# TensorE's unrolled program against a loop of 31 turns, in a gather-and-add kernel

## The chip, the cores and the metric

The kernel runs on one core of one Trainium2 chip. A core has TensorE (matrix products), VectorE (DVE in the profile), ScalarE (Activation, ACT), GpSimd (POOL) and SyncE (SP), each with its own instruction stream; semaphores order them. Sixteen DMA engines move data between the chip's memory (HBM) and the core's SBUF. The metric is the device time of one execution in microseconds, the median of several runs.

## The reference

```
x: (128, 128, 1024) f32     itok: (128,) int32, 0 to 7     weights: (8, 128, 128) f32
w = weights[itok]                                 # one matrix per batch
return x + einsum('bct,bcd->bdt', x, w)
```

For each of the 128 batches, a 128 x 128 matrix is chosen by the batch's subject, its transpose multiplies the batch's 128 x 1024 block, and the block is added. 67.1 MB are read and 67.1 MB written; the weights are 0.5 MB.

## The kernel before

A *slot* holds 4 batches (H * G, with H = 2 halves of G = 2 batches), 128 partitions by 4096 floats, 2 MB. There are SLOTS = 12 of them in SBUF, `xs[0]` to `xs[11]`, and NT = 32 fillings; filling i uses slot k = i % 12. All loops in the Python text are unrolled, so each engine's stream is a straight list.

The loads are issued from the ScalarE queue (`load`, through `transfer`, L59), one per batch, with 16 KB packets. From filling 12 on, ScalarE first waits until the slot's former content has been stored. The stores are issued from the SyncE queue (`store`), one per slot, but one per half in the first and last filling. The very last batch is stored by a transfer of its own, `last`, after the main block.

The work between is in halves, j = 0 to 63. For each half:

- GpSimd reads the subjects into registers (every 16 batches), waits until VectorE has added half j - 2 and, except in the first two halves, until the half's load has landed, and copies each batch's matrix from `w_all` into one of four small tiles `ws` (L202). For this it works out an address in a register, which the trace calls FUSED_REGOPS.
- TensorE waits until the semaphore `s_copied` has reached j + 1 and runs four matrix products of 128 x 512 outputs (L212), two per batch, into one of two PSUM tiles `ps`. The chip runs each f32 product as two pairs of weight load and matmul.
- VectorE waits for `s_product`, adds the half in PSUM to the half in the slot, in place (L223), and raises `s_added`.
- SyncE waits for `s_added` and issues the store.

In the first two halves TensorE also waits for the load itself. Before all this it runs three products on a tile of zeros (L152). The end (L235) waits on the ScalarE queue for the stores of the last 12 fillings.

A slot's place in the address of a matmul is a constant of the unrolled program. With 64 halves of four products, two pairs each, TensorE's stream has 512 weight loads and 512 matmuls of this kind, and each waits for `s_copied` at a constant that grows with j.

Of the kernel before, what the change touches and what calls it, by code (L numbers as in the profile page):

```python
# [30 lines left out]
G = 2  # L31
H = 2

N = 512

SLOTS = 12

W_SLOTS = 4
P_SLOTS = 2
# [12 lines left out]
def transfer(nc, engine, out, in_):  # L52

    later, nc._always_lower_symbolic_ap = nc._always_lower_symbolic_ap, False
    ins, outs = engine.lower_ap_dma(in_), engine.lower_ap_dma(out)
    nc._always_lower_symbolic_ap = later
    return engine.add_instruction(  # L59
        mybir.InstDMACopy(  # L60
            name=nc.get_next_instruction_name(),
            engine=engine.engine,
            ins=ins,
            outs=outs,
            mode="Copy",
            cce_op=ALU.bypass,
            queue=QUEUES[engine.engine],
        )
    )


@with_exitstack
def kernel(
    ctx: ExitStack,
    tc: tile.TileContext,
    x: bass.AP,
    subjects: bass.AP,
    weights: bass.AP,
    out: bass.AP,
):  # L80
    nc = tc.nc
    B, C, T = x.shape
    S, _, D = weights.shape
    NT = B // (G * H)

    def sbuf(name, *shape, dtype=F32):
        return ctx.enter_context(nc.sbuf_tensor(name, list(shape), dtype)).ap()


    room = -(nc.sbuf_base + -nc.sbuf_base % 32) % ALIGN  # L90
    if room:
        sbuf("room", C, room // 4)
    xs = [sbuf(f"x{i}", C, H * G, T) for i in range(SLOTS)]
    given, near, wrap, index = (
        sbuf(name, 1, B, dtype=I32) for name in ("given", "near", "wrap", "index")
    )
    w_all = sbuf("w_all", C, S, D)
    ws = [sbuf(f"w{i}", C, 1, D) for i in range(W_SLOTS)]
    zeros = sbuf("zeros", C, N)
    ps = [  # L100
        ctx.enter_context(nc.psum_tensor(f"ps{i}", [D, G, T], F32)).ap() for i in range(P_SLOTS)
    ]

    s_given = tc.alloc_semaphore("s_given")
    s_wall = tc.alloc_semaphore("s_wall")
    s_index = tc.alloc_semaphore("s_index")
    s_zeros = tc.alloc_semaphore("s_zeros")
    s_copied = tc.alloc_semaphore("s_copied")
    s_product = tc.alloc_semaphore("s_product")
    s_added = tc.alloc_semaphore("s_added")  # L110

    s_pair = [[tc.alloc_semaphore(f"s_pair{i}_{h}") for h in range(H)] for i in range(SLOTS)]


    s_first = tc.alloc_semaphore("s_first")

    def emptied(i, h):

        turns = i // SLOTS
        return (DMA * G + (DMA if h == H - 1 else 0)) * turns  # L120

    def loaded(i, q):

        h = q // G
        return s_pair[i % SLOTS][h], emptied(i, h) + DMA * G

    def load(engine, i, q):
        k, h = i % SLOTS, q // G
        transfer(
            nc,  # L130
            engine,
            xs[k][:, q, :],
            x[i * H * G + q].rearrange("(a r) t -> a (r t)", r=ROWS),
        ).then_inc(s_pair[k][h], DMA)

    def store(i, q0, q1):
        k, b = i % SLOTS, i * H * G
        transfer(
            nc,
            nc.sync,  # L140
            out[b + q0 : b + q1].rearrange("g d t -> d g t"),
            xs[k][:, q0:q1, :].rearrange("d (o g) t -> d o (g t)", g=min(G, q1 - q0)),
        ).then_inc(s_first if i == 0 and q1 == G else s_pair[k][(q1 - 1) // G], DMA)

    with tc.tile_critical():  # L145

        nc.sync.dma_start(given, subjects.rearrange("(o b) -> o b", o=1)).then_inc(s_given, DMA)

        nc.vector.memset(zeros, 0.0).then_inc(s_zeros, 1)  # L149
        nc.tensor.wait_ge(s_zeros, 1)  # L150
        for _ in range(IDLE):
            nc.tensor.matmul(  # L152
                ps[P_SLOTS - 1][:, G - 1, :N], zeros[:, :D], zeros, start=True, stop=True
            )

        nc.vector.wait_ge(s_given, DMA)
        nc.vector.tensor_scalar(near, given, -S, S - 1, ALU.max, ALU.min).then_inc(s_index, 1)  # L159
        nc.vector.wait_ge(s_index, 1)  # L160
        nc.vector.tensor_scalar(wrap, near, 0, S, ALU.is_lt, ALU.mult).then_inc(s_index, 1)  # L161
        nc.vector.wait_ge(s_index, 2)
        nc.vector.tensor_tensor(index, near, wrap, ALU.add).then_inc(s_index, 1)  # L163
        nc.gpsimd.wait_ge(s_index, 3)


        nc.scalar.dma_start(w_all, weights.rearrange("s c d -> c s d")).then_inc(s_wall, DMA)  # L167
        for i in range(NT):
            k = i % SLOTS
            if i == SLOTS:  # L170
                nc.scalar.wait_ge(s_first, DMA)
            if i >= SLOTS:
                nc.scalar.wait_ge(s_pair[k][H - 1], emptied(i, H - 1))
            for q in range(H * G):
                load(nc.scalar, i, q)


        for j in range(NT * H):
            i, q0, q1 = j // H, j % H * G, (j % H + 1) * G
            k = i % SLOTS  # L180
            p = ps[j % P_SLOTS]

            ahead = j < P_SLOTS
            if ahead:
                nc.tensor.wait_ge(*loaded(i, q0))
            for q in range(q0, q1):
                b = i * H * G + q
                if b % R == 0:  # L190
                    _, subject = nc.values_load_multi_w_load_instructions(
                        index[0:1, b : b + R],
                        engines=[mybir.EngineType.Pool],
                        min_val=0,
                        max_val=S - 1,
                        skip_runtime_bounds_check_because="the index is clamped on the chip above",
                    )
                if b == 0:
                    nc.gpsimd.wait_ge(s_wall, DMA)
                if not ahead and q == q0:  # L200
                    nc.gpsimd.wait_ge(s_added, j - P_SLOTS + 1)
                copy = nc.gpsimd.tensor_copy(  # L202
                    ws[b % W_SLOTS], w_all[:, bass.ds(subject[b % R], 1), :]
                )
                if not ahead and q == q0:
                    copy.wait_op(*loaded(i, q0), "sem-ge")
            copy.then_inc(s_copied, 1)

            nc.tensor.wait_ge(s_copied, j + 1)
            for q in range(q0, q1):  # L210
                for t in range(0, T, N):
                    mm = nc.tensor.matmul(  # L212
                        p[:, q % G, t : t + N],
                        ws[(i * H * G + q) % W_SLOTS][:, 0, :],
                        xs[k][:, q, t : t + N],
                        start=True,
                        stop=True,
                    )
            mm.then_inc(s_product, 1)

            mine = xs[k][:, q0:q1, :]
            nc.vector.wait_ge(s_product, j + 1)
            nc.vector.tensor_tensor(  # L223
                mine, p, mine, ALU.add
            ).then_inc(s_added, 1)

            if i == 0 or q1 == H * G or i == NT - 1:
                nc.sync.wait_ge(s_added, j + 1)
                store(i, q0 if i in (0, NT - 1) else 0, q1 - (b == B - 1))

    with tc.tile_critical() as waits:
        for i in range(NT - SLOTS, NT):
            nc.scalar.wait_ge(s_pair[i % SLOTS][H - 1], emptied(i + SLOTS, H - 1))  # L235
        nc.scalar.wait_ge(s_pair[(NT - 1) % SLOTS][0], emptied(NT - 1 + SLOTS, 0) + DMA)
    last = nc.sync.dma_start(out[B - 1], xs[(NT - 1) % SLOTS][:, H * G - 1, :])

    tc.add_manual_dep(
        last.ins,  # L240
        waits.name,
        mybir.DependencyInfo(mybir.DependencyClass.NoSync, mybir.DependencyReason.SCHED_ONLY),
        reason="the end of the program waits for it",
    )
# [27 lines left out]
```

## Time and profile before

| | us |
|---|---|
| median of 3 runs | 325.33 (325.26 to 325.57) |
| the profiled execution, its own time | 325.08 |
| its span, first to last instruction | 323.3 |
| TensorE matmul busy | 239.6 (74%), 518 instructions |
| VectorE busy | 147.9 (46%) |
| GpSimd busy | 34.0 (11%) |

| DMA queue | packets in the span | MB |
|---|---|---|
| q10, loads (ScalarE queue) | 7184 | 67.64 |
| q1, stores (SyncE queue) | 8882 | 67.11 |
| q8, instructions | 4 | 0.07 |
| q14, instructions | 4 | 0.03 |

The profile is of one execution. Its time is 1.8 us more than its span, which counts from the program's first instruction to its last. Matmuls are pipelined, so a busy TensorE is not TensorE at its peak. The page cuts the span into 40 slices of 8.1 us and gives the busy share of each in tenths. "DMA" is the mean over the 16 DMA engines. [...] The trace also holds each DMA packet with its queue, size, start and duration, but not the number of its engine.

### The profile page before, as it was taken

How to read it: one execution, taken by the hardware profiler on the slowest of the kernel's cores; microseconds unless marked ns; L12 is line 12 of the kernel's file. 1: busy time of each engine (PE TensorE's matmuls, PEld its weight loads, DVE VectorE, ACT ScalarE, POOL GpSimd, SP SyncE). 2: the span in 40 equal slices, each digit the busy share in tenths (PEclk: the TensorE clock that was granted, in tenths of full speed). 3: DMA queues.
4: the chain of work that ended last, by engine and by line, in shares of the span. 5: the costliest groups of instructions: out<-in, count | busy, mean ns of one | idle time of the engine just before them, and what ended most of it. 6: DMA issues, size and time to landing. Idle time of an engine off the chain costs nothing.

```text
span 323.3 us, 1608 instructions
## 1 busy us (share of the span) xinstructions
PE 239.6 (74%) x518; PEld 94.5 (29%) x518; DVE 147.9 (46%) x68; POOL 34.0 (11%) x132
## 2 busy tenths in 40 slices
PE   6999988998888888888889988888888587000000
PEld 2444433333333333333333333333333232000000
DVE  1375655555555555555555555555555355000000
POOL 1011111111111111111111011111111010000000
PEclk9999999999999999999999999999999999555555
DMA  7999999999999999999999999999999999999996
GB/s 270 430 381 423 436 419 423 426 428 428 431 423 425 434 415 427 428 429 420 432 430 418 428 425 428 423 430 429 419 435 416 424 427 427 427 424 429 429 423 276
DMA packets 16074, 134.85 MB, mean 417 GB/s; under 512 B 2625, under 2 KB 3650, under 8 KB 3906
## 3 DMA queue, kind: packets, MB, share of 16 engines
q10 hardware_dynamic: 7184, 67.64, 49.9%
q1 hardware_dynamic: 8882, 67.11, 49.3%
q8 instruction: 4, 0.07, 0.1%
q14 instruction: 4, 0.03, 0.0%
HBM read 67.63 MB, written 67.11 MB: 417 GB/s over the span
## 4 chain that ended last, share of the span: by engine, by line
PE 41%; DVE 20%; issue 17%; POOL 4%; DMA 2%; POOLq 1%; ACTq 0%; SPq 0%
PE ps L212 41%; DVE x L223 20%; POOL w L202 4%; DMA x<-in_x_dram 2%; POOLq L202 1%; ACTq L59 0%; ACTq L167 0%; ACTq L268 0%; SPq L145 0%
## 5 line engine op out<-in xcount | busy, mean ns | idle before, releaser
L212 PE MATMUL ps<-x,w 128*128 128x512 f32 x512 | 234.7, 604 | 31.6 <-POOL w L202 30.0
L223 DVE TENSOR_TENSOR x<-ps,x 128x2048 f32<-128x2048 f32 x64 | 146.7, 2292 | 125.4 <-PE ps L212 125.4
L212 PEld LDWEIGHTS ps<-x,w 128*128 128x128 f32 x512 | 92.6, 189 | 173.8 <-issue 92.3
L202 POOL COPY w<-w_all 128x128 f32 x128 | 33.8, 294 | 234.8 <-DMA x<-in_x_dram 204.5
L152 PE MATMUL ps<-zeros 128*128 128x512 f32 x6 | 4.9, 978 | 1.7 <-DVE zeros L149 1.7
L152 PEld LDWEIGHTS ps<-zeros 128*128 128x128 f32 x6 | 1.8, 326 | 3.8 <-issue 2.1
L149 DVE MEMSET zeros<- 128x512 f32 x1 | 0.5, 485 | 1.1 <-SPq L145 1.1
L159 DVE TENSOR_SCALAR near<-given 1x128 int32<-1x128 int32 x1 | 0.2, 216 | 0.6 <-DMA given<-in_itok_B_dram 0.6
L163 DVE CUSTOM_DVE_ANT_0 index<-near,wrap 1x256 uint16<-1x256 uint16 x1 | 0.3, 278 | 0.0
L161 DVE TENSOR_SCALAR wrap<-near 1x128 int32<-1x128 int32 x1 | 0.2, 215 | 0.0
L259 POOL MEMSET const-float32-0.0<- 128x1 f32 x1 | 0.1, 99 | 0.2 <-issue 0.2
L259 POOL MEMSET const-bfloat16-1.0<- 128x1 bf16 x1 | 0.1, 102 | 0.0
L259 POOL MEMSET const-uint8-127<- 128x1 uint8 x1 | 0.1, 102 | 0.0
L259 POOL MEMSET const-float32-1.0<- 128x1 f32 x1 | 0.1, 99 | 0.0
## 6 DMA issues: line engine op xcount, KB each, us to landing
x<-in_x_dram ACTq DMA_DIRECT2D x128, 512.0 KB, 32.0
out_dram<-x SPq DMA_DIRECT2D x30, 2048.0 KB, 47.2
out_dram<-x SPq DMA_DIRECT2D x3, 1024.0 KB, 14.0
out_dram<-x SPq DMA_DIRECT2D x2, 512.0 KB, 21.2
w_all<-in_L_cond_weights_dram ACTq DMA_DIRECT2D x1, 512.0 KB, 4.2
given<-in_itok_B_dram SPq DMA_DIRECT2D x1, 0.5 KB
```

The costliest lines, as they stand in the source:

```text
L149: nc.vector.memset(zeros, 0.0).then_inc(s_zeros, 1)
L152: nc.tensor.matmul(ps[P_SLOTS - 1][:, G - 1, :N], zeros[:, :D], zeros, start=True, stop=True)
L159: nc.vector.tensor_scalar(near, given, -S, S - 1, ALU.max, ALU.min).then_inc(s_index, 1)
L161: nc.vector.tensor_scalar(wrap, near, 0, S, ALU.is_lt, ALU.mult).then_inc(s_index, 1)
L163: nc.vector.tensor_tensor(index, near, wrap, ALU.add).then_inc(s_index, 1)
L202: copy = nc.gpsimd.tensor_copy(ws[b % W_SLOTS], w_all[:, bass.ds(subject[b % R], 1), :])
L212: mm = nc.tensor.matmul(p[:, q % G, t : t + N], ws[(i * H * G + q) % W_SLOTS][:, 0, :], xs[k][:, q, t : t + N], start=True, stop=True,)
L223: nc.vector.tensor_tensor(mine, p, mine, ALU.add).then_inc(s_added, 1)
L259: nc = _bacc.Bacc("TRN2", target_bir_lowering=False, num_devices=1)
```

## The change

The slots become one tile `x_all` of 12 slots, and `xs[i]` are views of it, so that a slot's place can be an offset. The matmuls of a half move into a function `multiply(slot, q0, q1)`. It is called with a constant slot for the first filling, where the two waits for a load stand ahead of it, and in a loop on TensorE, `Fori(1, NT)`, for the 31 others, with the slot `turn % SLOTS` in a register. A turn is one filling: two halves, eight matrix products. Because a wait in a loop cannot grow with j, TensorE now waits until `s_copied` is at least 1 and takes one off it.

The loop stands after the unrolled text of the other engines, whose streams keep their order; each engine's stream gets one more branch at the seam. In TensorE's stream the built program shows, per turn: one register move, two separate semaphore instructions, eight fused register operations (one ahead of each product), the eight products, one addition and one compare-and-branch.

```diff
-    xs = [sbuf(f"x{i}", C, H * G, T) for i in range(SLOTS)]
+    x_all = sbuf("x_all", C, SLOTS * H * G * T)
+    xs = [
+        x_all[:, i * H * G * T : (i + 1) * H * G * T].rearrange("c (q t) -> c q t", t=T)
+        for i in range(SLOTS)
+    ]
...
+    def multiply(slot, q0, q1):
+        p = ps[q0 // G % P_SLOTS]
+
+        nc.tensor.wait_ge(s_copied, 1).then_inc(s_copied, -1)
+        for q in range(q0, q1):
+            for t in range(0, T, N):
+                at = slot * (H * G * T) + (q * T + t)
+                mm = nc.tensor.matmul(
+                    p[:, q % G, t : t + N],
+                    ws[q % W_SLOTS][:, 0, :],
+                    x_all[:, bass.ds(at, N)],
+                    start=True,
+                    stop=True,
+                )
+        mm.then_inc(s_product, 1)
...
-            nc.tensor.wait_ge(s_copied, j + 1)
-            for q in range(q0, q1):
-                for t in range(0, T, N):
-                    mm = nc.tensor.matmul(
-                        p[:, q % G, t : t + N],
-                        ws[(i * H * G + q) % W_SLOTS][:, 0, :],
-                        xs[k][:, q, t : t + N],
-                        start=True,
-                        stop=True,
-                    )
-            mm.then_inc(s_product, 1)
+            if i == 0:
+                multiply(0, q0, q1)
...
+        with nc.tensor.Fori(1, NT) as turn:
+            for h in range(H):
+                multiply(turn % SLOTS, h * G, (h + 1) * G)
```

## The prediction

> **What bounds the kernel now.** I read the page's slices first, to see which resource is full and until when.
>
> ```profile
> PE   6999988998888888888889988888888587000000
> DMA  7999999999999999999999999999999999999996
> GB/s 270 430 381 423 436 419 423 426 428 428 431 423 425 434 415 427 428 429 420 432 430 418 428 425 428 423 430 429 419 435 416 424 427 427 427 424 429 429 423 276
> q8 instruction: 4, 0.07, 0.1%
> q14 instruction: 4, 0.03, 0.0%
> ```
>
> The 16 DMA engines are full from the second slice to the last but one, at about 427 GB/s, while TensorE stops six slices (48 us) before the end. What follows TensorE's stop is a backlog of stores. So the bytes over the rate set the time, and TensorE matters only if it lets the queues run dry. Next the waits, for what TensorE itself waits on.
>
> ```profile
> POOL w L202 <- DMA x<-in_x_dram: 204.5, 55, 6.8
> DVE x L223 <- PE ps L212: 125.4, 64, 8.8
> PE ps L212 <- POOL w L202: 30.0, 55, 3.7
> ```
>
> GpSimd, which copies the weight matrices for TensorE, waits for loads 55 times, 204.5 us in all; TensorE waits for GpSimd. Compute is paced by the loads, and DMA is the bound from both sides. Last the end of the span in stretches (columns: stretch, its length, busy time and count of PE, PEld, DVE, POOL, the clock, DMA share, GB/s).
>
> ```profile
> 314.00:318.00 4.00, 0.00 (x0) 0.00 (x0) 0.00 (x0) 0.00 (x0) 0.50 1.01 424
> 318.00:320.00 2.00, 0.00 (x0) 0.00 (x0) 0.00 (x0) 0.00 (x0) 0.50 0.99 408
> 320.00:321.00 1.00, 0.00 (x0) 0.00 (x0) 0.00 (x0) 0.00 (x0) 0.50 0.46 188
> 321.00:322.00 1.00, 0.00 (x0) 0.00 (x0) 0.00 (x0) 0.00 (x0) 0.50 0.11 45
> ```
>
> The engines do not end together: at 320 us all are busy, a microsecond later few are. **The end is set by the last DMA engine, not by the mean**, and this is where a change in TensorE's program can reach it: instruction blocks are fetched by the same engines.
>
> **What the packet records say of that.** Every transfer ends on each of the 16 engines with a 4-byte semaphore packet. For the last store these 16 end at 320.03, 320.04, 320.05, 320.19, 320.24, 320.27, 320.46, 320.56, 320.61, 320.67, 320.81, 320.83, 321.29, 321.44, 321.49 and 321.86 us. Twelve lie within 0.8 us, four are 0.5 to 1.0 us behind these. The four packets of the q8 queue are 16,384 bytes each, start at 47.61, 114.61, 181.85 and 248.85 us and take 954 to 1036 ns, where a load's packet of that size takes 616. By 47.61 us, 193 weight loads and matmuls of TensorE have started, by the others 449, 705 and 961: steps of 256, so q8 is the fetch of TensorE's unrolled program, a block per 256 instructions of 64 bytes. After the first, exactly one engine is late: the second-to-last of the store that lands next ends at 55.09, the last at 56.39. From the end backwards a packet follows its predecessor on an engine without a gap, and every engine carries the same sequence of packet sizes, so I can tell the engines apart. The four fetches lie on four different engines, and these are the four that end last (47.6 on the one that ends at 321.49, 114.6 on 321.44, 181.9 on 321.29, 248.8 on 321.86).
>
> **The change part by part.**
>
> *Removed: the four fetches.* TensorE's program falls from 1053 instructions to 109 in the built program, under one block of 256. What a fetch costs its engine: two engines that were on time in the early loads and met no fetch end at 320.03; two like them with a fetch at 321.44 and 321.29. That is 1.41 and 1.26 us. The latest engine was also 1.1 us late in the early loads (36.04 against 34.9 us for the same load); its like without a fetch, 36.09 there, ends at 320.56, so its fetch cost 321.86 − 320.56 = 1.30 us. Without the fetches the four would end at 320.0 to 320.6, and the last would be the engine that carries two of the four small q14 fetches (8,192 bytes, 309 ns each, other engines' programs): 320.83. The end moves by 321.86 − 320.83 = 1.03 us. The bounds: at least the freed work spread evenly, 4 × 0.616 / 16 = 0.15 us, where another execution's last engine carries no fetch; at most 1.3 us, one whole fetch. I take 1.03, since this execution shows it. After the last packet, 1.4 us of semaphore waits and barriers follow to the end of the span; Activation's wait for the store before it moves by as much, since the same engine was last there.
>
> *Added in the loop, per turn (two halves of a slot):* eight fused register operations, two separate waits that also take one off the semaphore, a register move and an addition, a compare-and-branch. The nearest row is GpSimd's, which does the same kind of operation before every copy:
>
> ```profile
> L202 POOLq FUSED_REGOPS  x108: 46/46/46, 41.7 to 268.5; - x108
> L202 POOL COPY w<-w_all x108: 293/294/295, 43.3 to 268.8; 128x128 f32 x108
> ```
>
> At 46 ns eight are 0.37 us. TensorE's sequencer may be slower: its semaphore instruction takes 51 ns in the trace where GpSimd's takes 17, three times, so 138 ns and 1.10 us is the upper bound. The two waits are 2 × 51 = 0.10 us, the branch 0.17 (the branch at TensorE's start takes 168 ns), the move and the addition 0.09 to 0.28. Together 0.73 to 1.65 us a turn. Most lies under the matmuls in the queue: a half's four matrix products run 3.71 us in the chain, and only the first operation after each wait is bare, about 2 × (51 + 46 to 138) = 0.2 to 0.4 us a turn. Even with nothing hidden a turn is 2 × 3.71 + 1.65 = 9.1 us.
>
> *What hides it.* Turns 1 to 31 run from 14.3 us to the last product at 276, 8.45 us each, paced by the loads. The queues run dry only if the last product comes after about 316 us (its store needs 5 us): (316 − 14.3) / 31 = 9.7 us a turn. So 9.1 costs nothing. If the cover were gone, each 0.1 us a turn over 9.7 would cost 3.1 us.
>
> *Moved or unchanged.* Queued behind the new wait are that half's weight loads and matmuls; GpSimd and VectorE wait for these, with the same cover. The first slot is not in the loop, so the first store is issued as before (14.19 us); it matters, as loads alone slow from 612 to 948 ns a packet at 17 us, until stores join. The big tile has the slots' bytes in the same order, and the 165 transfers have the same sizes. The other engines get a branch or two (33 to 47 ns), beside a queue that holds 19 us or more of stores: nothing.
>
> [...] The trace shows taken branches of TensorE only at its start, with no q8 packet near them. [...]
>
> **The rivals.**
>
> *Every turn fetches.* One mechanism: the jump back makes the sequencer load its block again. 31 fetches instead of 4, 1.3 us each, two on most engines: a late-started engine would end at 320.56 + 2 × 1.3 = 323.2, 1.3 us later than now, so 326.6; and with a stall above 2.3 us a turn (9.7 − 7.4) the loss grows by 31 us for each further microsecond. Against it: block steps fall at starts 193, 449 and so on, at least 205 instructions into the program with those ahead of the first product, while the loop lies between instruction 55 and 102. Chance 0.10.
>
> *Register operands slow TensorE itself.* If each of a turn's eight products cost over (9.7 − 7.42) / 8 = 0.29 us more, in the open, TensorE would become the bound; at 0.35, 0.5 us a turn over the limit, 15 us, 340. GpSimd's copies behind a register operation keep 294 ns, which speaks against it. Chance 0.06.
>
> *The last engine is not usually that late.* The late start and the last fetch met on one engine here. Where they do not, the end is a fetch alone, about 321.4, and falls to 320.83: 0.5 to 0.6 us, 324.8, which a measurement cannot tell from no change (0.2%, 0.65 us, is the bound I use). A change that fails to remove the fetches' effect, because other blocks are fetched at the seam, ends here too. For it: four engines were late at the start and only one of them got a fetch. Against: the median of 325.33 lies above this execution. Chance 0.24.
>
> **How the numbers follow.** The profiled execution took 325.08 us, 1.8 outside its span of 323.3. Less 1.03 is 324.05. The median lies 0.25 above that execution; carried over, 325.33 − 1.03 = 324.3, the forecast, chance 0.60. Its own range is 323.9 to 324.7. Faster by more than 0.2% is under 324.68, so 0.60; the small gain is "same", 0.24; the first two rivals are slower, 0.16. The range goes from 323.8 (1.3 us plus the spread work of 0.15) to 325.9 (nothing gained, and something of the seam), and leaves the slower cases out.
>
> **What would show it.** Right: no q8 packet in the span, 16 engines of the last store within about 0.9 us and the last near 320.8, TensorE's turn still about 8.3 us with loads as what GpSimd waits for. The first rival shows as q8 packets by the dozen, the second as GpSimd waiting for VectorE instead of loads and a DMA row with holes. The forecast is wrong if the last engine is as late without any fetch, for then lateness comes from the start.

## The result and the profile after

The changed kernel took 324.26 us (324.0 to 324.8, 12 runs) against 325.27 (325.0 to 325.69, 12 runs) for the kernel before, taken beside it: a ratio of 0.9972, 95% interval 0.9965 to 0.9980, or 1.0 us (0.65 to 1.14) less. The forecast was 324.3.

The slices of the changed kernel's page, as before: TensorE's and the DMA engines' busy tenths, the rate, and the one instruction queue that is left.

```profile
PE   6999988988888888888898888888888788000000
DMA  7999999999999999999999999999999999999996
GB/s 252 428 399 422 421 426 430 424 426 422 433 420 427 428 426 425 427 421 428 429 423 424 428 431 416 428 432 423 422 434 417 426 423 428 427 427 424 427 427 287
q14 instruction: 4, 0.03, 0.0%
```

There is no q8 line: TensorE fetches no block within the span. The DMA engines are as full as before, and TensorE still stops well ahead of the end. Then the waits of the changed kernel.

```profile
POOL w L222 <- DMA x_all<-in_x_dram: 204.3, 55, 5.2
DVE x_all L234 <- PE ps L156: 126.3, 64, 8.9
```

GpSimd waits for loads as often and as long as before (55 times; 204.3 us against 204.5). Compute is still paced by the loads. Last the end of the span in stretches, with DMA share and rate in the last two columns.

```profile
314.00:318.00 4.00, 0.00 (x0) 0.00 (x0) 0.00 (x0) 0.00 (x0) 0.50 1.00 421
318.00:320.00 2.00, 0.00 (x0) 0.00 (x0) 0.00 (x0) 0.00 (x0) 0.50 1.02 420
320.00:321.00 1.00, 0.00 (x0) 0.00 (x0) 0.00 (x0) 0.00 (x0) 0.50 0.36 143
321.00:322.00 1.00, 0.00 (x0) 0.00 (x0) 0.00 (x0) 0.00 (x0) 0.50 0.03 12
```

The tail is shorter: between 320 and 322 us the engines are busy 0.39 us on the mean, before 0.57. The packet records show who is left. The 16 ends of the last store are 319.98 to 320.56 for thirteen engines, then 320.94, 320.99 and 321.48 us. Where four engines trailed the rest by 0.5 to 1.0 us, one trails so far now. It carries GpSimd's two small fetches and was late from the first loads on. (These q14 fetches are at 62.2 and 192.8 us, when GpSimd has started 71 and 199 instructions: 128 apart, so a packet of 8,192 bytes is 64 bytes an instruction, as TensorE's 16,384 bytes for 256 were before.)

This execution took 324.63 us, among the slower of the twelve, which fall into seven of 324.00 to 324.31 and five of 324.57 to 324.80. So the two profiled executions differ by 0.45 us, the medians by 1.0. The profiles show what went, the runs show what it was worth.

What the loop costs TensorE stands in the trace of its line (duration in ns, least, median and most) and of the loop's own line:

```profile
L156 PEldq FUSED_REGOPS  x248: 46/46/103, 15.2 to 270.3; - x124
L242 PEldq COMPARE_BRANCH  x31: 76/208/223, 19.3 to 270.6; - x31
```

From the end of GpSimd's copy to TensorE's first weight load of a half it was 52 ns before, and is now 329 in a slot's first half and 284 in its second (medians), 0.51 us more a turn. In exchange for that, four blocks of instructions are not fetched.

### The profile page after: what moved, and what is told of

It reads as the page before. It is cut to its first block, busy times and chain, and to the rows that moved or that the text cites. A ratio compares the mean times of both kernels' runs of the same rounds, so it can differ in the third digit from the quotient of the medians.

```text
span 322.9 us, 2012 instructions
## 1 busy us (share of the span) xinstructions
PE 241.8 (75%) x518; PEld 94.8 (29%) x518; DVE 147.9 (46%) x68; POOL 34.2 (11%) x132
## 5 line engine op out<-in xcount | busy, mean ns | idle before, releaser
L156 PE MATMUL ps<-x_all,w 128*128 (+1 forms) x512 | 236.3, 607 | 30.3 <-PEq L152 29.1
L234 DVE TENSOR_TENSOR x_all<-ps,x_all 128x2048 f32<-128x2048 f32 x64 | 146.7, 2292 | 126.3 <-PE ps L156 126.3
L156 PEld LDWEIGHTS ps<-x_all,w 128*128 128x128 f32 x512 | 92.9, 191 | 174.4 <-issue 174.4
L222 POOL COPY w<-w_all 128x128 f32 x128 | 34.0, 296 | 235.3 <-DMA x_all<-in_x_dram 204.3
```

What stands on the lines that cost most here:

```text
L156: mm = nc.tensor.matmul(p[:, q % G, t : t + N], ws[q % W_SLOTS][:, 0, :], x_all[:, bass.ds(at, N)], start=True, stop=True,)
L222: copy = nc.gpsimd.tensor_copy(ws[b % W_SLOTS], w_all[:, bass.ds(subject[b % R], 1), :])
L234: nc.vector.tensor_tensor(mine, p, mine, ALU.add).then_inc(s_added, 1)
```

## The experiments

The theory: each block that TensorE fetches makes one DMA engine late by about 1.3 us, and since only the last engine counts, one fetch costs nearly as much as four. The rivals: the one tile or the new waits made the gain; the cost is a sum over the fetches; a turn over 8.45 us already delays the end; every jump back fetches.

The experiments were run in two sets, on two chips, each with the kernel before beside it: 325.09 us in the first set, 325.05 in the second, about 0.2 less than beside the change. So an expected time is best read by its difference from the kernel before. The changed kernel itself was not run again in either set; its ratio of 0.9972 is carried over from the result. In the second set the kernel with five products, which fetches nothing either, shows the gain too (0.9980).

**Everything but the loop.**

```diff
-            if i == 0:
-                multiply(0, q0, q1)
+            multiply(k, q0, q1)
...
-        with nc.tensor.Fori(1, NT) as turn:
-            for h in range(H):
-                multiply(turn % SLOTS, h * G, (h + 1) * G)
```

> The change without its loop: one tile for all slots, the separate waits that take one off the semaphore, but all 32 fillings unrolled with constant addresses. Fetch theory (the last DMA engine is late by the fetches of TensorE's program): four q8 packets as before, four late engines, 325.2 to 325.5, as before. Rival (the one tile or the new waits made the gain): 324.1 to 324.5, as with the change.

Measured: 325.00 us against 325.09 of the kernel before beside it, ratio 1.000 (0.9991 to 1.0010). The interval does not touch that of the change. The tile and the waits gain little or nothing; the gain is the loop's.

```profile
q8 instruction: 3, 0.05, 0.1%
```

Three blocks fall in the span, at 85.7, 170.7 and 233.2 us, the first after 20 halves, where the kernel before had its first after 11; so a count of 256 instructions alone does not say where a block is fetched. The fourth packet, which had been expected among them, came at 325.05, after the program's last instruction. It may still cost something: in this kernel alone the time outside the span goes up to 2.28 us (median 1.97), where all the others have 1.72 to 1.85. By the spans alone the medians are 323.05 against 323.3 us, 0.25 less with one fetch fewer, about a quarter of the gain. The three engines that fetched are the three that end last, at 321.78 and twice 322.19; the others end by 321.11.

**One fetch.**

```diff
-            if i == 0:
-                multiply(0, q0, q1)
+            if i < 8:
+                multiply(k, q0, q1)
...
-        with nc.tensor.Fori(1, NT) as turn:
+        with nc.tensor.Fori(8, NT) as turn:
```

> Eight fillings unrolled, the other 24 in the loop, so that TensorE passes one block boundary. Both theories expect one q8 packet, near 47 us. Last-engine theory: one engine is late by 1.3 us, and as only the last one counts, most of the four fetches' cost is back: 324.9 to 325.2. Rival (what counts is the sum of the fetched bytes or of the engines' time): a quarter of the cost, 324.5.

Measured: 324.75 us against 325.09, ratio 0.9989 (0.9981 to 0.9998).

```profile
q8 instruction: 1, 0.02, 0.0%
```

By the sum, three quarters of the gain would be left, a ratio of 1 - 0.75 x 0.0028 = 0.9979, just outside the interval; with the least gain that the result allows, 0.0020, it would be 0.9985 and inside it, so this run alone does not decide. The last-engine theory's 324.9 to 325.2 is 0.9987 to 0.9996 of the 325.33 that it was worked out from, and the measured ratio lies in that. The fetch had been expected near 47 us and came at 72.2, in the loop's first turn. It made its engine end at 321.47, where eight engines end at 319.93 to 320.05. So it costs 1.4 to 1.5 us here, with no late start. In this execution it is not the last engine, though: another ends at 322.29, whose first load packet took 2599 ns in place of 611 at 4.3 us.

**The loop's body across a block boundary.**

```diff
-            if i == 0:
-                multiply(0, q0, q1)
+            if i < 5:
+                multiply(k, q0, q1)
...
-        with nc.tensor.Fori(1, NT) as turn:
-            for h in range(H):
-                multiply(turn % SLOTS, h * G, (h + 1) * G)
+        with nc.tensor.Fori(5, NT - 1, 2) as turn:
+            for m in range(2):
+                for h in range(H):
+                    multiply((turn + m) % SLOTS, h * G, (h + 1) * G)
+        for h in range(H):
+            multiply((NT - 1) % SLOTS, h * G, (h + 1) * G)
```

> Five fillings unrolled, then 13 turns of two fillings whose body of about 90 instructions lies across the block boundary, then the last filling unrolled. [...] If a jump back over a boundary fetches (the first rival of the prediction): 13 to 26 q8 packets, one or two on each engine, 325.5 to 327, and gaps ahead of TensorE's first weight load of a turn.

Measured: 325.11 against 325.09, ratio 0.9998 (0.9989 to 1.0007).

```profile
q8 instruction: 1, 0.02, 0.0%
```

One fetch, at 48.3 us, in the loop's first turn, and none at the 12 jumps back after it. Its engine is the last, at 321.98; an engine that was as late in the first loads and met no fetch ends at 320.52. With one fetch, the whole gain is gone; the sum's 0.9979 is outside this interval by more than before, and so is 0.9985. Where the boundary lies in the body can't be read from the trace, so whether each turn crossed it stays open here; the next experiment doesn't leave that open.

**A body longer than a block.**

```diff
-        with nc.tensor.Fori(1, NT) as turn:
-            for h in range(H):
-                multiply(turn % SLOTS, h * G, (h + 1) * G)
+        with nc.tensor.Fori(1, NT - 1, 10) as turn:
+            for m in range(10):
+                for h in range(H):
+                    multiply((turn + m) % SLOTS, h * G, (h + 1) * G)
+        for h in range(H):
+            multiply((NT - 1) % SLOTS, h * G, (h + 1) * G)
```

> One filling unrolled, then 3 turns of ten fillings (a body of over 400 instructions, so that it lies in two or three blocks of 256), then the last filling. If TensorE keeps the blocks of the whole body, each block is fetched once: one or two q8 packets, 324.7 to 325.2. [...]

Measured: 325.21 against 325.05, ratio 0.9999 (0.9990 to 1.0007).

```profile
q8 instruction: 2, 0.03, 0.0%
```

A body of over 400 instructions, over 25 KB at the 64 bytes worked out above, cannot lie in one block of 16,384 bytes, so every jump back crosses a boundary. The blocks come at 43.8 and 95.8 us. TensorE jumps back at 92.5 and 176.4 us; 3.3 us after the first a block comes, after the second none. So a jump back over a boundary does not fetch every time, and a turn over several blocks did not fetch them all again. Nor is there a gap after a jump: both times the first weight load follows GpSimd's copy by 0.335 us, in the changed kernel by 0.329. One or two packets had been expected if TensorE keeps the blocks of the whole body, and two came; but the second came 3.3 us after a jump back, so what it brought is not settled, and how many blocks are kept was not shown. Two fetches cost as much as four did, again by the last-engine theory. This kernel also runs 30 of its 32 fillings in a loop, with the register operations of the change, and has no gain: so it is not the loop's timing on TensorE that gains.

**Twice the fetches.** The kernel before, with products of 256 columns:

```diff
-                for t in range(0, T, N):
+                for t in range(0, T, N // 2):
                     mm = nc.tensor.matmul(
-                        p[:, q % G, t : t + N],
+                        p[:, q % G, t : t + N // 2],
...
-                        xs[k][:, q, t : t + N],
+                        xs[k][:, q, t : t + N // 2],
```

> The kernel before with products of 256 columns instead of 512: twice as many weight loads and matmuls, eight fetches instead of four. Last-engine theory: each fetch falls on another engine, so eight engines are late by 1.3 us and the end hardly moves, 325.3 to 325.8, ratio to before 1.000 to 1.0015. Rival (the cost adds up over the fetches, 0.25 us each): 326.3, ratio 1.003. TensorE's turn grows by less than the cover of 1.3 us in both.

Measured: 325.25 against 325.09, ratio 1.0008 (0.9999 to 1.0016).

```profile
q8 instruction: 8, 0.13, 0.2%
```

Twice the fetches, and the end moves by 0.16 us, not clear of nothing; a sum of 0.25 us for each of four more, 1.003, is outside the interval. The eight fetches lie on eight engines, and these are the eight that end last, from 321.28 to 322.31; the others end from 319.84 to 321.23. More engines are late, the last hardly more than before (321.86).

**More work in a turn: five products, and six.** The last product of a half is made again, once or twice, with the same output; the second kernel has `* 2`.

```diff
+    def extra(slot, q0, q1):
+        made = [(q, t) for q in range(q0, q1) for t in range(0, T, N)]
+        return made + (made[-1:] * 1 if slot is not None and not isinstance(slot, int) else [])
...
-        for q in range(q0, q1):
-            for t in range(0, T, N):
+        for q, t in extra(slot, q0, q1):
+            if True:
```

> The changed kernel with the last product of each half in the loop made twice: five products in place of four, the same output. TensorE's half grows by about 0.87 us, so a turn needs at least 8.7 to 9.1 us, under the limit of 9.7 that the prediction worked out. Theory (DMA is the bound, TensorE has cover to 9.7): the same time as the changed kernel within 0.5 us, 324 to 324.8, with TensorE ending later. Rival (a turn over today's 8.45 us already delays the end): (8.9 - 8.45) x 31 = 14 us more.

Measured: 324.43 against 325.05, ratio 0.9980 (0.9971 to 0.9989), the same gain as the change. The waits and the slices of this kernel:

```profile
POOL w L226 <- DVE x_all L238: 237.2, 62, 8.6
PE   6999999999999999999999999999999999900000
DMA  7999999999999999999999999999999999999997
```

GpSimd now waits for VectorE, and so for TensorE, in 62 halves and no longer for the loads; TensorE is the slowest engine, full to 281.8 us where its last product ends (273.8 in the changed kernel). The last product is 8.0 us later and the gain is the same within the intervals, since the stores' backlog takes the delay; the rival would have had these 8 us at the end. A turn takes (281.8 - 14.3) / 31 = 8.6 us, a little less than the 8.7 that I had expected as the least.

> As the one with five, but six products in a half: a turn of at least 10.4 to 10.9 us, over the limit of 9.7. Theory: TensorE becomes the bound, the last product comes at 14.3 + 31 x 10.6 = 343 us, the end 7 us after it, 345 to 360 in all. Rival (the cover is larger than worked out): under 335.

Measured: 345.14 us (2 runs), ratio 1.0613 (1.0589 to 1.0637).

```profile
PE   5999999999999999999999999999999999999991
DMA  7999999999999999999999999999999999635565
GB/s 253 430 405 426 426 431 422 427 427 427 427 427 424 423 433 426 420 428 427 427 428 424 427 424 430 426 420 425 436 416 426 426 426 426 258 162 219 244 274 213
```

Now the DMA row has holes, from the 35th slice on. The last product ends at 336.7 us, (336.7 - 14.3) / 31 = 10.4 us a turn, and the last store 6.2 us later. All 16 engines end between 342.71 and 342.86: here, with idle time among the last stores, no engine's lateness is carried to the end.

**A try at the late start.** In the changed kernel, the first two loads ahead of the weights:

```diff
-        nc.scalar.dma_start(w_all, weights.rearrange("s c d -> c s d")).then_inc(s_wall, DMA)
...
                 load(nc.scalar, i, q)
+                if i == 0 and q == G - 1:
+                    nc.scalar.dma_start(
+                        w_all, weights.rearrange("s c d -> c s d")
+                    ).then_inc(s_wall, DMA)
```

> The changed kernel with the first two loads issued ahead of the load of the weights, in the same queue. In the profiles one or a few of the first 16 KB load packets, at 4 to 6 us, take 1.3 to 2.6 us in place of 0.61, right behind the 512-byte packets of the weights, and the engine that had the longest is among the last at the end. If the small packets ahead make the long ones, these go, the end comes up to 0.5 us earlier: 323.7 to 324.1. If the first large reads stall wherever they stand, there is no change: 324.1 to 324.5. TensorE starts within 1 us of 8.3 us in both.

Measured: 325.18 against 325.05, ratio 1.0008 (0.9994 to 1.0022), the runs from 324.5 to 327.0. Neither expectation holds: no load packet takes over 1.2 us any more, and yet the gain of the change is gone.

```profile
POOL w L225 <- DMA w_all<-in_L_cond_weights_dram: 9.0, 1, 9.0
```

GpSimd waits 9.0 us for the weights, where it waited 4.8: two loads ahead cost the weights 4.2 us, not the one that I had allowed for. The last store's engines spread from 319.90 to 321.92, with no TensorE fetch at all. So an engine can be as late where only the start differs, without a fetch by TensorE and without long packets; which of the first transfers makes it is not settled. This was the one try at a version faster than both, and it is not one.

## Why the prediction was right

*The four fetches go, and the end moves by one engine's lateness.* Right, and shown by runs that change little else: the unrolled stream with the new waits is as slow as before, or 0.25 us faster within its span; against the loop's gain of 0.9 us (by the ratio), one fetch takes back 0.6 us in one kernel and all of it in another, two take back all, and eight hardly more than all. In the profiled executions every engine that fetched is among the last, and the end of the last engine sets the time: in all ten but the unrolled kernel's (3.49), the time is 3.13 to 3.22 us more than that end. The forecast of 1.03 us, worked out from one execution, met a median of 1.0; that it fits so closely is luck, as the two profiled executions differ by 0.45. The step beneath it, that the engine with GpSimd's two small fetches would be last, at 320.83, was right on the engine and not on the size: in the profile after it ends at 321.48, as it had a late start too. So one sign of being right was missed: the 16 ends spread over 1.5 us, not 0.9. That meeting is a matter of the execution, and it is a likely reason for the two groups among the twelve runs, which I argue from one profile and did not show.

*1.3 us for a fetch.* Right within its spread: 1.4 to 1.5 us in the execution with one fetch and no late start.

*Three readings of the trace were off, and little hangs on them.* Four of the 16 ends that the prediction lists (320.05, 320.19, 320.24 and 320.61) belong to the store before the last: each is 1.25 us ahead of one of the four latest ends, on the same engine. The four in their place are 319.91 to 320.01, so twelve engines end within 0.9 us and the same four trail. Of the 193 weight loads and matmuls, 188 are such, and five are other instructions of TensorE; the steps of 256 stand. The last product ends at 272.8 us, not 276, so a turn was 8.3 us and not 8.45; it is 8.3 after the change too, and the limit of 9.7 does not use it.

*The loop's cost is hidden.* Right. The fused operations take GpSimd's 46 ns and not the 138 of the upper bound. The term for the bare part was too small: 0.2 to 0.4 us a turn forecast, 0.51 measured, for there is time between the wait, the first operation and the weight load that no instruction's duration shows. With the separate wait and constant addresses, in the unrolled kernel, the first weight load follows the copy by 114 ns; so most of the 329 and 284 comes with the register operations. It cost nothing, as the waits for loads took it.

*The limit of 9.7 us a turn.* Borne out from both sides: five products in a half (8.6 us a turn) were free, six, 10.4 us a turn, came to 345.14 us, at the lower end of its expectation of 345 to 360. The limit itself was not measured closer than between these two.

*Every turn fetches.* Did not occur: no q8 packet in the changed kernel. That a loop inside one block fetches nothing was my estimate, and no run ahead of the prediction showed it; these 31 turns show it for this loop. Of the two jumps back of the kernel with ten fillings in a turn, whose body is longer than a block, one was followed by a fetch.

*Register operands slow TensorE.* Did not occur: the median matmul is 592 ns before and after, and a half's eight, whose starts are 429 ns apart, so that they overlap, take 3.70 us in both.

*The last engine is not usually that late.* This rival was given 0.24. Its mechanism is there, with the roles changed: in the kernel after, it is GpSimd's fetches that a late start may meet. Five of the twelve runs lie at 324.57 to 324.80, near this rival's 324.8. It was not strong enough to bring the median's gain under 0.2%, but the interval reaches down to just that. The prediction's sign of being wrong, a last engine as late without any fetch, did not come in the changed kernel (321.48 against 321.86); it did in the kernel with the loads ahead (321.92), whose start differs. So lateness comes from the fetches and from the start, and the runs separate only the first.

## What to carry to other kernels

Where DMA is the bound, ask which of the 16 engines ends last, and what that engine did that the others did not; a share of the mean hides it. A fetched block of instructions is small in bytes (0.05% of the traffic here) and yet made one engine 1.3 to 1.5 us late here; one fetch cost most or all of what four did, so most of the gain comes only when the last one goes. A loop on an engine with cover was free here, but first work out how long a turn may become, from when its last product is needed.

## What the runs showed of the hardware

- A 16 KB block that TensorE fetches took 951 to 1036 ns beside full queues, a load's packet of that size 616; the eight blocks of the kernel with products of 256 columns went to eight different DMA engines, while GpSimd's two 8 KB blocks lay on one engine, before and after.
- The first load packets, at 4 to 6 us, took up to 2.6 us in place of 0.61 in the kernel with one fetch, and up to 1.57 in the kernel before. Where the queues stayed full, an engine's lateness from them was still there 315 us later (322.29 against 320.0 in the kernel with one fetch, part of it from a small fetch); with idle time among the last stores, in the kernel with six products, all 16 engines ended within 0.15 us.
- Loads alone slowed down to a mean of 0.74 to 0.95 us a packet in the two or three microseconds ahead of the first store's packets. Where the first store came 4 us later (the kernel with one fetch), the slow stretch came 4 us later too, at 20 to 21 us. The cause was not looked for.
